# A 3x3 convolution by four columns at a time, with six products each, in a fused convolution, attention and expert kernel

## The chip, the cores and the metric

The kernel runs on one core of one Trainium2 chip. All data is float32. The metric is the device time of one execution, in microseconds, as the median of several runs. The profile is that of one execution; its engines are TensorE (PE, with PEld for its weight loads), VectorE (DVE), ScalarE (ACT), GpSimd (POOL) and SyncE (SP), which only starts transfers.

## The reference

Eight images of 32 x 32 positions with 256 channels pass through two layers. The input of each is normalised first, and its output is added to the input. The first layer is a 3 x 3 convolution to 192 channels beside an attention of 8 heads with relative positions to 64 channels; the second is a plain attention of width 128; after both comes a layer of experts, two of eight per image. Cut to what the change touches:

```
conv_out = lax.conv_general_dilated(x, conv_w, window_strides=(1, 1), padding='SAME', ...) + conv_b
kqv = jnp.einsum('bhwc,co->bhwo', x, qkv_w) + qkv_b
...
return jnp.concatenate([conv_out, attn], axis=3)
...
def _gn(v, G=32, eps=1e-5):
    g = v.reshape(B_, H_, W_, G, C_ // G)
    m = jnp.mean(g, axis=(1, 2, 4), keepdims=True)
    s = jnp.var(g, axis=(1, 2, 4), keepdims=True)
    return ((g - m) / jnp.sqrt(s + eps)).reshape(v.shape)
```

The input of the first layer is normalised over groups of 8 channels (`_gn`). The order of positions matters only to the convolution and the relative positions; every other step treats a position by itself, or sums over all.

## The kernel before

An image is a tile `T` of 128 partitions x 8 tiles x 256 channels, positions on the partitions; two adjacent columns share a partition row (`load_image`, `j=2`). All layers add into `T`.

`norm_steps` transposes `T` to channels on partitions (`xT`), takes mean and variance per channel, averages them over groups by two tiny products, and writes the normalised image with a border of zeros into `gpad` (L319). `by_tiles` copies `gpad` tile by tile into `x` for the products that make the values (L340, GpSimd). `by_pairs` makes the inputs of the convolution: for each pair of output columns and each of two channel halves (`kc`) four differences or sums of neighbouring columns, into `gdif` (L331, two on VectorE and two on GpSimd). `conv_weights` makes four weight variants of the three column taps once, at the start (L273 to L278).

`conv_steps` then runs the convolution of an image as 4 row groups x 2 pairs x 2 variants x 6 products (3 rows x 2 channel halves), 96 calls. Two variants share one PSUM tile `pc`; after the second, VectorE adds them into `T` (first pair: L483 and two L487; second pair: L481). An f32 product is two records in the profile, so 8 images give 1536.

The convolution is a filler for TensorE. An image passes three stages:

- `conv_layer_attention` runs 32 steps of two score products each, per unit of four heads and half the queries. VectorE takes the row maxima of each score tile (`my`, L540, then L544, L547) from one of two PSUM buffers `lg`. After 8 steps of a unit, `fold` (L553 to L558) turns the maxima into a row of the operand `F` by a DMA. From step 10 (`lead = NT + LAG`) `weigh` (L572, then the exponential on ScalarE, L580) and `gather` (L589) run in the same steps. In the first ten steps, when there is nothing to weigh, `conv.run` spreads what is left of the image's calls evenly: `todo = -(-left // (lead - s))`, after a first portion of six.
- After step 32, `ahead` walks through the next image's `norm_steps`, `by_tiles` and `by_pairs`, while the last weights are still gathered. `settle` (L615 to L619) divides by the sums (`rc`, `at`), then come `aT` (L690), `pp` and its addition into `T` (L696).
- `attention_layer` is the second layer. Its `fill` runs `input_steps` of the next image in between (keys and queries `pk` and `kq`, L354 to L366; values `pvv`; the relative products `prel`, L426, with copies L438 and L440), and after each of eight small pieces six calls of the next image's convolution, in the single PSUM buffer `po`.

The order on TensorE is the written one throughout (`tc.manual_schedule`). In the start-up block VectorE's order is the written one as well: normalisation, key patterns, four input steps, `reld_steps`, `by_pairs`, the other input steps, the weights. Elsewhere a scheduler orders each queue at build time[...]. The experts' stage, from about 1985 us on, is not touched but for the shape of its output transfer.

## Time and profile before

| | us |
|---|---|
| median of 3 runs | 2483.72 (2482.58 to 2485.73) |
| the profiled execution | 2482.71 |
| its span, first to last instruction | 2480.2 |
| one image in the steady state (first score to first score) | 242.1 |
| first convolution product of the first image | 58.3 |
| mean granted TensorE clock | 0.984 of full speed |

A group line of the page gives line, engine, operation, output and inputs, shapes and count, then busy time and the mean length of one, then the engine's idle time ahead of it and what ended it. A timeline row gives start, length, engine, line, operation, shapes and how many instructions are merged in it, with the idle time ahead and its end in brackets. A row of busy times by stage gives the stretch, its length, then busy time and instruction count of PE, PEld, DVE, ACT and POOL, the granted clock, the share of the DMA engines and GB/s. A line of waits gives who waited for whom, the sum, the number and the longest.

### The profile page before, as it was taken

To read this page: it belongs to the slowest core of one execution; us is meant where nothing else is said; L and a number is where in the kernel's file an instruction comes from. 1 tells how busy PE (TensorE), PEld (TensorE's weight loads), DVE (VectorE), ACT (ScalarE), POOL (GpSimd) and SP (SyncE) were. 2 spreads that over 40 slices of the span, in tenths; PEclk is the share of its full clock that TensorE was granted. 3 is DMA by queue.
4 is the path that set the end of the run, shared out by engine and by line. 5 is a ranking of instruction groups with operands and counts; after the bars stand their busy time and mean duration, and the time that the engine had idled before them with its cause. 6 is when DMAs were issued, how large, how long until landed. Compare 5 with 4: busy or idle time off the path is not lost. (4 is left out here: it accounts for less than half of the span.)

```text
span 2480.2 us, 42408 instructions
## 1 busy us (share of the span) xinstructions
PE 2362.5 (95%) x17657; PEld 1359.1 (55%) x17657; DVE 1452.0 (59%) x2507; ACT 981.8 (40%) x1625; POOL 449.4 (18%) x463
## 2 busy tenths in 40 slices
PE   5999999999999999999999999999998869999998
PEld 4635753565366436643664376337632646666665
DVE  6774477448744874587368636864674444444443
ACT  1155326432543364336334622472256323322232
POOL 6003020302040103100320122021200132222221
PEclk8999999999999999999999999999999979999999
DMA  4520252024212312241224032402240032211110
GB/s 123 78 41 24 37 101 37 26 44 93 38 37 51 82 30 48 56 77 18 54 54 81 10 57 69 69 5 57 51 71 3 1 124 78 75 68 68 68 60 26
DMA packets 73774, 135.86 MB, mean 55 GB/s; under 512 B 12000, under 2 KB 24168, under 8 KB 71536
## 3 DMA queue, kind: packets, MB, share of 16 engines
q1 hardware_dynamic: 67792, 115.47, 22.7%
q0 software_dynamic: 3056, 15.73, 1.9%
q8 instruction: 139, 2.28, 0.4%
q10 hardware_dynamic: 2736, 1.97, 0.3%
q14 instruction: 51, 0.42, 0.1%
HBM read 53.43 MB, written 25.17 MB: 32 GB/s over the span
## 5 line engine op out<-in xcount | busy, mean ns | idle before, releaser
L580 ACT ACTIVATE PT<-st 128x512 f32<-128x512 f32 (+1 forms) x944 | 541.5, 633 | 580.6 <-PE st L572 576.7
L540 DVE TENSOR_REDUCE my<-lg 128x32 f32<-128x1024 f32 x512 | 617.5, 1222 | 159.7 <-PE st L572 126.5
L572 PE MATMUL st<-F,km 32*128 32x512 f32 x2048 | 550.6, 641 | 14.9 <-DMA F<-mb 8.7
L532 PE MATMUL lg<-km,F 24*128 24x512 f32 x2048 | 525.1, 636 | 0.3 <-issue 0.2
L589 PE MATMUL po<-PT,vall 128*32 128x256 f32 (+1 forms) x3200 | 315.0, 453 | 2.4 <-ACT PT L580 2.4
L472 PE MATMUL pc<-convw,gdif 128*128 128x192 f32 x1536 | 289.0, 337 | 9.7 <-DVE convw L276 6.2
L472 PEld LDWEIGHTS pc<-convw,gdif 128*128 128x128 f32 x1536 | 248.0, 191 | 75.1 <-issue 72.2
L532 PEld LDWEIGHTS lg<-km,F 24*128 24x128 f32 x2048 | 150.9, 183 | 174.3 <-issue 103.2
L589 PEld LDWEIGHTS po<-PT,vall 128*32 128x32 f32 x3200 | 67.0, 108 | 313.9 <-issue 279.9
L572 PEld LDWEIGHTS st<-F,km 32*128 32x128 f32 x2048 | 179.8, 184 | 93.4 <-issue 43.3
L1168 PE MATMUL py<-w,hT 128*128 128x256 f32 x1024 | 223.6, 379 | 0.0
L1151 PE MATMUL phd<-n2T,w 128*128 128x512 f32 x512 | 223.6, 594 | 0.0
L1168 PEld LDWEIGHTS py<-w,hT 128*128 128x128 f32 x1024 | 194.6, 190 | 33.3 <-issue 7.4
L299 POOL TENSOR_TENSOR T<-T,l0b 128x2048 f32<-128x2048 f32 x8 | 36.3, 4536 | 813.2 <-PE tpx L290 813.2
L1151 PEld LDWEIGHTS phd<-n2T,w 128*128 128x128 f32 x512 | 97.0, 191 | 114.8 <-issue 107.7
L1175 DVE TENSOR_TENSOR r<-py,n 128x256 f32<-128x256 f32 x64 | 27.1, 423 | 213.6 <-PE py L1168 213.6
L804 PE MATMUL po<-pt,qkv 128*128 128x256 f32 x512 | 116.6, 381 | 11.3 <-DVE pt L796 11.3
L1158 ACT ACTIVATE hT<-phd,b1c 128x512 f32<-128x512 f32 x128 | 86.3, 686 | 96.4 <-PE phd L1151 96.1
L782 DVE TENSOR_REDUCE nm<-lg 128x1 f32<-128x1024 f32 x64 | 78.2, 1221 | 77.8 <-PE lg L773 77.8
L773 PE MATMUL lg<-qkv 128*128 128x512 f32 x256 | 119.1, 593 | 0.0
L804 PEld LDWEIGHTS po<-pt,qkv 128*128 128x128 f32 x512 | 96.6, 190 | 36.2 <-DVE pt L796 13.2
L721 POOL TENSOR_TENSOR T<-T,n 128x256 f32<-128x256 f32 x64 | 47.2, 744 | 351.8 <-DVE n L716 351.8
(231 smaller groups left out, 2446.5 us busy)
## 6 DMA issues: line engine op xcount, KB each, us to landing
F<-rh SPq DMA_DIRECT2D x256, 128.0 KB
F<-kq SPq DMA_DIRECT2D x256, 64.0 KB
F<-rwd SPq DMA_DIRECT2D x256, 64.0 KB
w<-in_L_ffn_W_dram SPq DMA_DIRECT2D x32, 512.0 KB
rwd<-rw SPq DMA_DIRECT2D x16, 512.0 KB
Td<-T POOLq DMA_DIRECT2D x8, 1024.0 KB, 7.9
T<-Td SPq DMA_DIRECT2D x8, 1024.0 KB
out_dram<-yo SPq DMA_DIRECT2D x16, 512.0 KB
```

Of the source, the lines that this page charges most:

```text
L472: nc.tensor.matmul(pc[:, v, :], lhsT=gflat[:, 2 * pair + v, kc, at : at + P], rhs=convw[:, 2 * pair + v, dy, kc, :], start=i == 0, stop=i ...
L532: nc.tensor.matmul(lg[:, a, :], lhsT=self.F[r : r + 24, a, 0, i * P : (i + 1) * P], rhs=KM[self.g][r : r + 24, a].rearrange("p e k -> p (e ...
L540: nc.vector.tensor_reduce(my[:, :, hl], lg.rearrange("p a (y x) -> p y a x", y=WW), AX.XY, ALU.max)
L572: nc.tensor.matmul(st[:, i, :] if len(heads) > 1 else st, lhsT=KM[self.g][r : r + 32, a, e, :], rhs=self.F[r : r + 32, a, e, :], start=Tru ...
L580: nc.scalar.activation(self.pts[j][:, hs, :], st, AF.Exp)
L589: nc.tensor.matmul(self.po[32 * hl : 32 * hl + 32, cols], lhsT=vall[:, j, h * (DH + 1) : h * (DH + 1) + 32], rhs=self.pts[j][:, hl, cols], ...
L773: nc.tensor.matmul(lg[:, h, :], lhsT=qk[0][:, i * P : (i + 1) * P], rhs=qk[1][:, h * 512 : (h + 1) * 512], start=True, stop=True,)
L782: nc.vector.tensor_reduce(nm, lg, AX.X, ALU.max, negate=True)
L804: nc.tensor.matmul(po[:, 0:IB], lhsT=v1[:, jc, :], rhs=pt[:, jc, :], start=jc == 0, stop=jc == NT - 1)
L1151: nc.tensor.matmul(phd, lhsT=ws[k][0][:, kc, f * P : (f + 1) * P], rhs=n2T[:, kc, q * 512 : (q + 1) * 512], start=kc == 0, stop=kc == KC - 1,)
L1158: nc.scalar.activation(hT[:, k * NF + f, :], phd, AF.Gelu, bias=b1c[:, f, k * B + b : k * B + b + 1])
L1168: nc.tensor.matmul(py, lhsT=hT[:, k * NF + f, j * P : (j + 1) * P], rhs=ws[k][1][:, f, :], start=k == 0 and f == 0, stop=k == TOPK - 1 and ...
```

## The change

The convolution now makes four columns of outputs at a time from six products, where it made two from four; per image 2 row groups x 3 pairs x 2 variants x 6 products, 72 calls. The six weight variants and the six sums of columns have constants other than one, so that the sums are built by multiply-and-add (`scalar_tensor_tensor`) on VectorE and by additions on GpSimd, in two loops (`by_fours`): the first makes variants 0 and 1 out of 2 to 5 as scratch, the second fills 2 to 5 anew. The outputs of a pair of products go through a copy (`neg`) and a sum and difference (`sd`) before they are added to `T`.

Positions lie in tiles of every fourth column (`j=4` in the loads and stores), and the normalised image `x` is kept by columns without a border; the padded copy `gpad` and `by_tiles` are gone, and keys, queries and values read `x`. The order of the keys follows.

```diff
-                out=t.rearrange("p (r j) c -> p r j c", j=2), in_=xt[b].rearrange("(r p j) c -> p r j c", p=P, j=2)
+                out=t.rearrange("p (r j) c -> p r j c", j=4), in_=xt[b].rearrange("(r p j) c -> p r j c", p=P, j=4)
...
-        gpad = wp.tile([P, KC, HH + 2, WW + 2], FP, tag="gpad", name="gpad")
-        nc.gpsimd.memset(gpad, 0.0)
...
-        gdif = wp.tile([P, 4, KC, HH + 2, WW // 2], FP, tag="gdif", name="gdif")
+        NV, NQ = 6, WW // 4
+        gdif = wp.tile([P, NV, KC, HH + 2, NQ], FP, tag="gdif", name="gdif")
...
+            cw = [convw[:, v] for v in range(NV)]
+            nc.vector.tensor_tensor(cw[1], w0, w2, ALU.add)
+            nc.vector.tensor_tensor(cw[0], cw[1], w1, ALU.add)
+            nc.vector.tensor_tensor(cw[1], cw[1], w1, ALU.subtract)
+            nc.vector.tensor_scalar(convw[:, 0:2], convw[:, 0:2], -1.0 / 6, None, ALU.mult)
+            nc.vector.scalar_tensor_tensor(cw[3], w2, 4.0, w0, ALU.mult, ALU.add)
+            nc.vector.scalar_tensor_tensor(cw[2], w1, 2.0, cw[3], ALU.mult, ALU.add)
+            nc.vector.scalar_tensor_tensor(cw[3], w1, -2.0, cw[3], ALU.mult, ALU.add)
+            nc.vector.tensor_scalar(convw[:, 2:4], convw[:, 2:4], 1.0 / 24, None, ALU.mult)
+            nc.scalar.mul(cw[4], w0, 0.25)
+            nc.scalar.copy(cw[5], w2)
...
-                nc.vector.tensor_scalar(
-                    gpad[:, kc, 1 : HH + 1, 1 : WW + 1], xv, gm[:, kc, :], gr[:, kc : kc + 1], ALU.subtract, ALU.mult
-                )
...
+            xn = xn.rearrange("p (k a c j x) -> p k a c j x", k=KC, a=2, j=4, x=16)
             for kc in range(KC):
                 for a in range(2):
...
+                    nc.vector.tensor_scalar(
+                        xn[:, kc, a],
+                        xT[:, kc, a * 512 : (a + 1) * 512].rearrange("p (j x c) -> p c j x", j=4, x=16),
+                        gm[:, kc, :],
+                        gr[:, kc : kc + 1],
+                        ALU.subtract,
+                        ALU.mult,
+                    )
+            held["xn"] = xn
+
+        def by_fours(xn):
...
+            d = [[xn[:, kc, :, :, j].rearrange("p a c x -> p a x c") for j in range(4)] for kc in range(KC)]
+            v = [
+                [gdif[:, i, kc, 1 : HH + 1, :].rearrange("p (a x) c -> p a x c", a=2) for i in range(NV)]
+                for kc in range(KC)
+            ]
+
+            def stt(out, one, factor, two):
+                for a in range(2):
+                    nc.vector.scalar_tensor_tensor(out[:, a], one[:, a], factor, two[:, a], ALU.mult, ALU.add)
+
+            for d_, v_ in zip(d, v):
+
+                stt(v_[2], d_[1], -4.0, d_[3])
+                stt(v_[3], d_[0], -4.0, d_[2])
+                nc.gpsimd.tensor_tensor(v_[4], d_[3], d_[1], ALU.subtract)
+                nc.gpsimd.tensor_tensor(v_[5], d_[2], d_[0], ALU.subtract)
+                nc.gpsimd.tensor_tensor(v_[0], v_[2], v_[3], ALU.add)
+                nc.gpsimd.tensor_tensor(v_[1], v_[2], v_[3], ALU.subtract)
+            for d_, v_ in zip(d, v):
+
+                stt(v_[2], v_[5], 2.0, v_[4])
+                stt(v_[3], v_[5], -2.0, v_[4])
+
+                stt(v_[4], d_[1], -5.0, d_[3])
+                stt(v_[4][:, :, :, 1:NQ], d_[3][:, :, :, 0 : NQ - 1], 4.0, v_[4][:, :, :, 1:NQ])
+                nc.vector.tensor_scalar(v_[5], d_[0], 4.0, None, ALU.mult)
+                stt(v_[5], d_[2], -5.0, v_[5])
+                nc.gpsimd.tensor_tensor(
+                    v_[5][:, :, :, 0 : NQ - 1], v_[5][:, :, :, 0 : NQ - 1], d_[0][:, :, :, 1:NQ], ALU.add
+                )
...
-                    rhs=gpad[:, kc, 1 + 16 * q : 17 + 16 * q, 1 : WW + 1],
+                    rhs=xn[:, kc, q * 512 : (q + 1) * 512],
...
+            for r in range(2):
+                four = T[b][:, 4 * r : 4 * r + 4, 0:CO]
+                for pair in range(3):
...
+                                if pair < 2:
+                                    neg = work.tile([P, CO], FP, tag="neg", name="neg")
+                                    sd = work.tile([P, 2, CO], FP, tag="sd", name="sd", bufs=2)
+                                if pair == 0:
+                                    nc.scalar.copy(neg, pc[:, 1, :])
+                                    nc.vector.tensor_tensor(sd[:, 0], pc[:, 0, :], neg, ALU.add)
+                                    nc.vector.tensor_tensor(sd[:, 1], pc[:, 0, :], neg, ALU.subtract)
+                                    for h in range(2):
+                                        nc.gpsimd.tensor_tensor(
+                                            four[:, 2 * h : 2 * h + 2], four[:, 2 * h : 2 * h + 2], sd, ALU.add
+                                        )
+                                elif pair == 1:
+                                    nc.scalar.mul(neg, pc[:, 1, :], 2.0)
+                                    nc.vector.scalar_tensor_tensor(
+                                        sd[:, 0], neg, 0.5, pc[:, 0, :], ALU.mult, ALU.add
+                                    )
+                                    nc.vector.scalar_tensor_tensor(
+                                        sd[:, 1], pc[:, 0, :], 2.0, neg, ALU.mult, ALU.subtract
+                                    )
+                                    nc.gpsimd.tensor_tensor(four[:, 0:2], four[:, 0:2], sd, ALU.add)
+                                    nc.vector.scalar_tensor_tensor(
+                                        four[:, 2:4], sd, 4.0, four[:, 2:4], ALU.mult, ALU.add
+                                    )
+                                else:
+                                    nc.vector.tensor_tensor(four[:, 0:4:3], pc, four[:, 0:4:3], ALU.add)
...
-                self.left = 4 * NT // 2 * 3 * KC if b < B else 0
+                self.left = 2 * NV * 3 * KC if b < B else 0
...
-            by_pairs()
+            by_fours(held["xn"])
...
-                    yield from norm_steps(b + 1)
-                    held.update(by_tiles())
-                    by_pairs()
+                    yield from norm_steps(b + 1, held)
+                    by_fours(held["xn"])
```

More of the change, by code (lines that the diff above doesn't have):

```diff
@@ L271, in conv_weights, with norm_steps @@
             taps = taps.rearrange("p (a b n) -> p b a n", a=3, b=3)
-            convw = wp.tile([P, 4, 3, KC * CO], FP, tag="convw", name="convw")
-            nc.vector.tensor_tensor(convw[:, 2], taps[:, 0], taps[:, 2], ALU.add)
-            nc.vector.tensor_tensor(convw[:, 0], convw[:, 2], taps[:, 1], ALU.add)
-            nc.vector.tensor_tensor(convw[:, 1], convw[:, 2], taps[:, 1], ALU.subtract)
-            nc.vector.tensor_scalar(convw[:, 0:2], convw[:, 0:2], 0.5, None, ALU.mult)
-            nc.scalar.copy(convw[:, 2], taps[:, 0])
-            nc.scalar.mul(convw[:, 3], taps[:, 2], -1.0)
+            w0, w1, w2 = (taps[:, i] for i in range(3))
+            convw = wp.tile([P, NV, 3, KC * CO], FP, tag="convw", name="convw")
+            cw = [convw[:, v] for v in range(NV)]
[9 more added lines that the diff above has]
+            nc.scalar.copy(cw[5], w2)
             return convw.rearrange("p v a (k o) -> p v a k o", o=CO)
-        def norm_steps(b):
+        def norm_steps(b, held):
             xT = pt_tile("xT").rearrange("p (k s) -> p k s", k=KC)
@@ L290, in norm_steps @@
                     nc.tensor.transpose(tp[:, t, :], T[b][:, t, kc * P : (kc + 1) * P], ident)
-                nc.vector.tensor_copy(
-                    xT[:, kc, :].rearrange("p (r t j) -> p r j t", r=4, j=2), tp.rearrange("p (r j) t -> p r j t", j=2)
-                )
+                nc.vector.tensor_copy(xT[:, kc, :], tp.rearrange("p t k -> p (t k)"))
                 for q in range(2):
@@ L316, in norm_steps @@
             nc.vector.reciprocal(gr, gr)
-            for kc in range(KC):
-                xv = xT[:, kc, :].rearrange("p (h w) -> p h w", w=WW)
-                nc.vector.tensor_scalar(
-                    gpad[:, kc, 1 : HH + 1, 1 : WW + 1], xv, gm[:, kc, :], gr[:, kc : kc + 1], ALU.subtract, ALU.mult
-                )
-        def by_pairs():
-            for kc in range(KC):
-                d = [gpad[:, kc, 1 : HH + 1, j : j + WW - 1 : 2] for j in range(4)]
-                for v, (one, two, op) in enumerate(
-                    ((1, 2, ALU.add), (2, 1, ALU.subtract), (0, 2, ALU.subtract), (1, 3, ALU.subtract))
-                ):
-                    eng = nc.vector if v < 2 else nc.gpsimd
-                    eng.tensor_tensor(gdif[:, v, kc, 1 : HH + 1, :], d[one], d[two], op)
@@ L333, in by_tiles @@
-        def by_tiles():
             xn = f_tile("x").rearrange("p a e s -> p (a e s)")[:, 0 : KC * S]
-            xn = xn.rearrange("p (k j t) -> p k j t", k=KC, j=NT)
+            xn = xn.rearrange("p (k a c j x) -> p k a c j x", k=KC, a=2, j=4, x=16)
             for kc in range(KC):
                 for a in range(2):
-                    for e in range(4):
-                        nc.gpsimd.tensor_copy(
-                            xn[:, kc, a * 4 + e].rearrange("p (y x) -> p x y", y=8),
-                            gpad[:, kc, 1 + 16 * a : 17 + 16 * a, 1 + 8 * e : 9 + 8 * e],
-                        )
-            return dict(xn=xn)
+                    nc.vector.tensor_scalar(
[6 more added lines that the diff above has]
+                    )
@@ L346, in input_steps @@
         def input_steps(b, held):
+            xn = held["xn"].rearrange("p k a c j x -> p k (a c j x)")
             kq = work.tile([P, S], FP, tag="kq", name="kq")
@@ L363, in input_steps @@
                 nc.scalar.activation(
-                    kq[qs, q * 512 : (q + 1) * 512], pk[qs], AF.Identity, bias=kqbs[qs], scale=kqs[qs]
-                )
-                nc.vector.tensor_scalar(
-                    kq[0:DK, q * 512 : (q + 1) * 512].rearrange("p (e y x) -> p x e y", e=4, y=8),
-                    pk[0:DK].rearrange("p (x e y) -> p x e y", e=4, y=8),
-                    kqb[0:DK],
-                    None,
-                    ALU.add,
-                )
+                    kq[qs, q * 512 : (q + 1) * 512].rearrange("p (x y) -> p x y", y=WW),
+                    pk[qs].rearrange("p (y x) -> p x y", y=WW),
+                    AF.Identity,
+                    bias=kqbs[qs],
+                    scale=kqs[qs],
+                )
+                nc.vector.tensor_scalar(kq[0:DK, q * 512 : (q + 1) * 512], pk[0:DK], kqb[0:DK], None, ALU.add)
             for g in range(NG):
@@ L388, in input_steps @@
                         pv[:, j, :],
-                        lhsT=held["xn"][:, kc, j, :],
+                        lhsT=xn[:, kc, j * P : (j + 1) * P],
                         rhs=qkvw[:, kc, 2 * DK : 3 * DK],
@@ L463, in conv_steps @@
             n = 3 * KC
-            for r in range(NT // 2):
-                both = T[b][:, 2 * r : 2 * r + 2, 0:CO]
-                for pair in range(2):
+            for r in range(2):
+                four = T[b][:, 4 * r : 4 * r + 4, 0:CO]
+                for pair in range(3):
                     pc = place[0]("pc")[:, 0 : 2 * CO].rearrange("p (v o) -> p v o", v=2)
@@ L470, in conv_steps @@
                             dy, kc = divmod(i, KC)
-                            at = (8 * r + dy) * (WW // 2)
+                            at = (16 * r + dy) * NQ
                             nc.tensor.matmul(
@@ L479, in conv_steps @@
                             if v and i == n - 1:
-                                if pair:
-                                    nc.vector.tensor_tensor(both, pc, both, ALU.add)
-                                else:
-                                    nc.vector.tensor_tensor(
-                                        both, both, pc[:, 0:1, :].to_broadcast([P, 2, CO]), ALU.add
-                                    )
-                                    for j, op in enumerate((ALU.add, ALU.subtract)):
-                                        nc.vector.tensor_tensor(both[:, j], both[:, j], pc[:, 1, :], op)
+                                if pair < 2:
+                                    neg = work.tile([P, CO], FP, tag="neg", name="neg")
+                                    sd = work.tile([P, 2, CO], FP, tag="sd", name="sd", bufs=2)
@@ L606, in close @@
                 nc.scalar.copy(
-                    self.os.rearrange("p (r j t) -> p r j t", r=2, j=2),
-                    self.po.rearrange("p (r t j) -> p r j t", r=2, j=2),
+                    self.os.rearrange("p (j t) -> p j t", j=4), self.po.rearrange("p (t j) -> p j t", j=4)
                 )
@@ L898 @@
             half_w, half_h, reld_steps = tables()
-            for _ in norm_steps(0):
+            for _ in norm_steps(0, held):
                 pass
-            held.update(by_tiles())
             KM = key_patterns()
@@ L923, in ahead @@
                 def ahead():
-                    yield from norm_steps(b + 1)
-                    held.update(by_tiles())
-                    by_pairs()
+                    yield from norm_steps(b + 1, held)
+                    by_fours(held["xn"])
                 now, held = held, {}
@@ L1184 @@
             nc.sync.dma_start(
-                out=ot[b, q * 512 : (q + 1) * 512, :].rearrange("(r p j) c -> p r j c", p=P, j=2),
-                in_=y.rearrange("p (r j) c -> p r j c", j=2),
+                out=ot[b, q * 512 : (q + 1) * 512, :].rearrange("(p j) c -> p j c", j=4),
+                in_=y,
             )
```

## The prediction

> **What bounds the kernel now.** I read the page first, then the busy time by stage, the waits of single stages, and the timelines of VectorE and GpSimd where the change falls. The page:

> ```profile
> PE 2362.5 (95%) x17657; PEld 1359.1 (55%) x17657; DVE 1452.0 (59%) x2507; ACT 981.8 (40%) x1625; POOL 449.4 (18%) x463
> L472 PE MATMUL pc<-convw,gdif 128*128 128x192 f32 x1536 | 289.0, 337 | 9.7 <-DVE convw L276 6.2
> ```

> TensorE looks like the bound, at 95%, and the convolution (L472) has 1536 of its records, two for each f32 product. But "busy" stretches over waits inside a pipelined group, and the share is a mean over stages. An image takes 242 us, and its convolution is spent in two places: half fills the attention layer before (48 calls), half fills the ten steps in which only scores run (the lead: 560 to 594 us for the second image, 62 to 106 us for the first, which has all 96 calls there). By stage (columns: length, then busy time of PE, PEld, DVE, ACT, POOL):

> ```profile
> 62.00:106.00 44.00, 43.78 (x266) 32.98 (x264) 33.03 (x47) 0.00 (x0) 0.00 (x0) 0.99 0.50 68
> 560.00:594.00 34.00, 33.87 (x181) 20.08 (x182) 30.74 (x46) 1.49 (x2) 13.35 (x17) 1.00 0.41 100
> 691.00:708.00 17.00, 14.78 (x100) 4.12 (x92) 5.70 (x10) 14.48 (x21) 10.65 (x20) 1.00 0.00 0
> ```

> The second row matters most: in a later lead VectorE works 30.74 of 34.00 us. The waits of that stretch say who waits:

> ```profile
> PEld lg L532 <- DVE my L540: 4.4, 10, 0.8
> DVE my L540 <- PE lg L532: 2.2, 5, 0.6
> ```

> The score products wait for the maxima (L540) to free their two buffers more than the reverse. So the later leads are nearly bound by VectorE; only the first, with 33.03 of 44, is bound by TensorE. The tail of the attention, where the next image is normalised:

> ```profile
> 692.58 1.54 DVE L319 TENSOR_SCALAR gpad<-xT,gm,gr 128x1024 f32<-128x1024 f32 x2
> 694.03 2.97 DVE L331 TENSOR_TENSOR gdif<-gpad 128x512 f32<-128x512 f32 x4
> 706.86 0.26 DVE L618 RECIPROCAL rc<-pa 128x16 f32<-128x16 f32 x1 [9.85 <-PE pa L615]
> 707.15 0.29 DVE L619 TENSOR_TENSOR at<-pa,rc 128x128 f32<-128x128 f32 x1
> 707.36 1.48 DVE L690 COPY aT<-tpa 64x512 f32<-64x512 f32 x2
> ```

> From the start of the normalisation to the reciprocal (L618) VectorE has 706.86 - 692.58 = 14.28 us, 9.85 of them idle. From L618 on TensorE, in its written order, stands behind VectorE (at, aT, then pp). This is the cover that new VectorE work may use up. Start-up:

> ```profile
> 28.03 5.59 DVE L238 TENSOR_TENSOR reld<-bdh 128x192 f32<-128x192 f32 x8
> 33.54 4.32 DVE L331 TENSOR_TENSOR gdif<-gpad 128x512 f32<-128x512 f32 x4
> 37.78 1.06 DVE L366 TENSOR_SCALAR kq<-pk,kqb 64x512 f32<-64x512 f32 x1
> 38.69 0.66 DVE L395 TENSOR_TENSOR vall<-pvv,vb 128x512 f32<-128x512 f32 x1
> 39.28 1.87 DVE L438 COPY rw<-prel 128x512 f32<-128x512 f32 x2
> ```

> Here VectorE's order too is the written one: whatever the differences cost is passed to the rw copies, to the products after them, and to the first convolution at 58.25 us.

> [...]in the last stage four STT, 0.48 us each alone, took 2.15 us each beside GpSimd additions:

> ```profile
> 2073.12 8.60 DVE L1181 SCALAR_TENSOR_TENSOR yo<-r,fmv,T 128x256 f32<-128x256 f32 x4
> 2076.42 2.53 POOL L1141 TENSOR_TENSOR n<-n,bias 128x1024 f32<-128x1024 f32 x1
> ```

> That is one VectorE instruction per GpSimd instruction. [...]L547, reading 128 elements in steps of 16 bytes, takes 381 ns, L544 with 128 contiguous ones 293.[...]

> **The change part by part.**

> *Products.* 96 calls an image become 72: 24 x 2 records x 8 = 384 records fewer. A record costs 0.172 us (12 of them between 232.64 and 234.70 us in TensorE's timeline), so 8.26 us an image, 66 us in all, if TensorE were everywhere the bound. The attention layer still runs eight times six calls, so all 24 go from the lead, whose calls after the first six go from 42 to 18.

> *The later leads (seven).* VectorE's part of the convolution there was 3.5 us (L481 2 x 0.55, L483 2 x 0.55, L487 4 x 0.34). Left are one middle pair (two STT of 192 from PSUM, 0.41 each from L820's 0.479 for 256, and one of 384 in SBUF, 0.61 from L1180's 0.484 plus 128 ns) and one last pair (0.55): 2.0. But the old last pair came behind the fold (L553 to L558), whose DMA opens the next stage; the new one falls in front of it. Up to the fold VectorE goes from 2.9 to 2.0, less 0.3 for waits beside GpSimd's token sum. I take -0.6 an image, -4 in all; bounds -2 each (if TensorE's remaining stalls go too) and +0.5.

> *The first lead.* TensorE's step falls from 1.07 + 9 x 0.344 = 4.2 us to 3.3; VectorE's step (two maxima 2.36, folding 0.33, evictions about 0.55, gaps) is 3.4 to 3.6. -6 rather than -8.3. The four further weight operations (4 x 1.36 as L273 to L276, 5.4 us more on VectorE) lie beside the 5.6 us that it waited before its first maximum at 63.73, and cost nothing while the first pair waits only for its own two variants; otherwise +5.

> *Tail.* Removed: two L319, four L331, and on GpSimd 16 copies (6.6 us) and four differences. Added on VectorE: four TENSOR_SCALAR of 512 reading every eighth element, about 0.57 (L319 has 0.77 for 1024), 2.3; 28 STT of 128 elements. An STT of 128 is L1180's 0.484 - 0.128 = 0.36, 0.29 from start to start; 20 of them read d, in steps of 256 bytes, at 0.38; two TENSOR_SCALAR 0.35 each. Own time 2.3 + 8 x 0.29 + 20 x 0.38 + 0.7 = 12.9 us. GpSimd: eight additions of 256 in the first loop at 0.73 (L721) and two at the end. Now in order: at 3.8 us the first four STT are done beside the first two GpSimd ones; six more GpSimd ones at 0.78 go to 8.6, and let six STT through; left are 6 x 0.29 + 12 x 0.38 + 0.7 = 7.0, and one wait of 0.6: 16.2 us. Cover 14.28: L618 comes 1.9 us late, and TensorE with it. Six images like this, and the first pass with 15.8 of cover (449.00 to 464.76) 0.4: +12. Lower bound 0[...]; upper about 6 each, 40 in all[...].

> *Start-up.* The first eight STT go from 33.5 to 36.6. GpSimd's key patterns, ahead in its queue, end near 37 (41.3 less 4.4 for the copies that go); four additions to 39.9, and only then may the second loop overwrite. It ends near 49.5 (3.0 with one STT per GpSimd operation, 2.6, and 3.8 for the other half) where it ended at 37.8: +11 with L366's contiguous form 0.4 shorter. Bounds +6 and +14.

> *Attention layer.* A first or middle pair frees the single po buffer after one ScalarE copy (0.32) and two VectorE operations (0.7 to 0.8), about what three took before (1.2); a middle pair had 0.55. The 1.5 us of prel and tpn products between calls cover that, where ScalarE isn't in a copy. +1, bounds -2 and +7. GpSimd's additions into T come behind its own T additions; the DMA shapes (4 KB runs for 2 KB) wait for nothing here.

> *Sum:* 11 - 6 - 4 + 12 + 1 = +14. On the profiled execution (2482.71 us, its span 2480.2) 2496.7; the runs' median is 1.0 above it: 2498.

> **Rivals.**

> *The differences weigh more* (2533): stall 5.9 in six tails and 4.4 in one (+40), start-up +14, leads 0, first lead -6, layer +1: +49. For it: 28 small strided instructions beside ten GpSimd ones. Against: GpSimd's copies beside L331 barely slowed it (0.74 for 0.69).

> *The cover holds* (2468, faster): VectorE finishes within 14.28 us of the normalisation's start, so tails cost 0; start-up +6, first lead -8, seven leads -2: -16. It decides if the 28 STT average under 0.40 us as issued, waits included: (14.28 - 2.3 - 0.7) / 28. For it: 9.85 us idle; against: L1181.

> *Products count in full* (2418): all 66 us. For it: the 95%. Against: the waits in the later leads.

> **How the numbers follow.** Chances: my forecast 0.48 (own range 2487 to 2512), heavier 0.17, cover holds 0.25, full 0.06, else 0.04. The range 2466 to 2532 leaves out half of the heavier case, the full one and a little of each other. About 0.2% (5 us) is what a measurement of this kernel tells from no change. Faster: nearly all of cover and full, less their edge, 0.27; within: 0.13; slower: 0.60.

> **What would show it.** Later leads about as long as before with VectorE over 93% busy; L618 late and its idle time before it gone; the first convolution near 69 us; the first lead 6 us shorter. Wrong, if the leads shrink by several us each (then TensorE did bound them), or if VectorE is idle again before L618.

## The result, and the profile after

The kernel after the change takes 2580.01 us (median of 4 runs, 2577.76 to 2585.70) against 2484.64 us before: a ratio of 1.0388, 95% interval 1.0370 to 1.0407. It is slower, by nearly seven times the difference that was forecast. The profiled execution took 2577.76 us, with a span of 2576.0, so 95.8 us more span than before. The page of the kernel after:

```profile
PE 2423.9 (94%) x17273; PEld 1361.3 (53%) x17273; DVE 1532.9 (60%) x2703; ACT 992.2 (39%) x1657; POOL 503.2 (20%) x430
...
PEclk6999989998999799969996999699989879999999
...
L571 PE MATMUL lg<-km,F 24*128 24x512 f32 x2048 | 596.0, 735 | 6.7 <-DVE my L579 6.6
L611 PE MATMUL st<-F,km 32*128 32x512 f32 x2048 | 579.5, 671 | 15.5 <-DMA F<-mb 10.2
L494 PE MATMUL pc<-convw,gdif 128*128 128x192 f32 x1152 | 250.2, 364 | 7.5 <-DVE convw L276 6.3
```

The records of the convolution are down from 1536 to 1152, as they should be. But TensorE is busy for 61 us *more* (2423.9 against 2362.5), and the products that the change doesn't touch are longer: a score product (L571, L532 before) takes 735 ns on average where it took 636, a product of the weights' scores (L611) 671 where it took 641. The row PEclk says why: the granted clock dips in each of images 2 to 8, to 6 or 7 tenths in four of them. Its mean is 0.924 of full speed, 0.984 before. One image of each kernel by stage; in a row stand the length, then the busy time (and records) of PE, PEld, DVE, ACT, POOL, then the granted clock, the DMA share and GB/s. After, from the first score product of the fifth image: lead, steady stage, tail (from the next image's normalisation to its key products), the attention layer up to its own query and key products, and the rest of that layer.

```profile
1085.36:1125.17 39.81, 39.30 (x129) 19.62 (x130) 28.89 (x40) 1.82 (x3) 14.30 (x18) 0.57 0.35 84
1125.17:1229.54 104.37, 103.20 (x805) 37.34 (x802) 73.15 (x99) 61.14 (x109) 4.57 (x1) 0.94 0.27 43
1229.54:1251.24 21.70, 16.88 (x100) 7.30 (x101) 18.65 (x38) 12.92 (x19) 11.23 (x10) 0.92 0.00 1
1251.24:1290.40 39.16, 38.70 (x681) 33.42 (x681) 16.37 (x43) 10.20 (x18) 14.89 (x14) 0.96 0.35 68
1290.40:1344.72 54.32, 51.32 (x239) 36.27 (x237) 25.49 (x56) 19.64 (x34) 1.11 (x2) 1.00 0.21 33
```

The same image before:

```profile
1044.20:1077.92 33.72, 33.63 (x179) 19.84 (x178) 30.46 (x45) 1.49 (x2) 13.35 (x17) 1.00 0.40 100
1077.92:1176.76 98.84, 97.69 (x801) 34.88 (x802) 72.58 (x98) 60.91 (x109) 4.54 (x1) 1.00 0.28 45
1176.76:1194.20 17.44, 15.22 (x100) 5.67 (x100) 6.22 (x10) 12.93 (x19) 10.63 (x20) 1.00 0.01 2
1194.20:1231.94 37.74, 37.10 (x681) 32.77 (x681) 17.00 (x43) 9.45 (x15) 10.40 (x9) 1.00 0.34 72
```

The lead has 50 TensorE records fewer (48 by the code) and is 6 us longer; the steady stage has the same work on every engine and is 5.5 us longer. In both the clock has gone down, and no other column has grown to match. The stages of all images summed, in us:

| | start to first score | 8 leads | 7 steady stages | 7 tails | 7 layers, first part | second part | rest | span |
|---|---|---|---|---|---|---|---|---|
| before | 62.4 | 280.2 | 691.8 | 123.6 | 266.0 | 380.2 | 676.0 | 2480.2 |
| after | 72.3 | 292.4 | 724.9 | 149.5 | 276.4 | 380.2 | 680.3 | 2576.0 |
| difference | +9.9 | +12.2 | +33.1 | +25.9 | +10.4 | 0 | +4.3 | +95.8 |

The trace's records of the granted clock have two values, 1.0 and 0.5. Around the fourth and fifth image (start and length in us, factor):

```
before   946 to 1287: always 1.0
after    841.5  37.5  0.5    lead and steady stage of image 4
         879.0 109.2  1.0
         988.3   6.8  0.5    tail of image 4
         995.1  95.6  1.0
        1090.7  47.8  0.5    lead and steady stage of image 5
        1138.4 109.2  1.0
        1247.7   6.8  0.5    tail of image 5
```

The leads whose clock was low for long (images 4 to 7) are 37.4 to 39.8 us long, those where it was low only in the last ten us or less (images 2, 3 and 8) 32.7 to 33.1, where before had 33.8. In all seven VectorE runs the same instructions in the same order. So the theory to be tested: the convolution in the lead was not only work, it kept TensorE's clock up. With 18 calls left of 42 the clock falls to half there and stays low into the next stage. Its rival: VectorE's added work is the loss, and the low clock only mirrors a TensorE that waits.

### The profile page after: what moved, and what is told of

Its sections match the earlier page's. It is cut to its first block, busy times and chain, and to the rows that moved or that the text cites. A ratio compares the mean times of both kernels' runs of the same rounds, so it can differ in the third digit from the quotient of the medians.

```text
span 2576.0 us, 41839 instructions
## 1 busy us (share of the span) xinstructions
PE 2423.9 (94%) x17273; PEld 1361.3 (53%) x17273; DVE 1532.9 (60%) x2703; ACT 992.2 (39%) x1657; POOL 503.2 (20%) x430
## 5 line engine op out<-in xcount | busy, mean ns | idle before, releaser
L619 ACT ACTIVATE PT<-st 128x512 f32<-128x512 f32 (+1 forms) x944 | 543.1, 633 | 531.6 <-PE st L611 521.4
L571 PE MATMUL lg<-km,F 24*128 24x512 f32 x2048 | 596.0, 735 | 6.7 <-DVE my L579 6.6
L611 PE MATMUL st<-F,km 32*128 32x512 f32 x2048 | 579.5, 671 | 15.5 <-DMA F<-mb 10.2
L628 PE MATMUL po<-PT,vall 128*32 128x256 f32 (+1 forms) x3200 | 320.8, 461 | 2.9 <-ACT PT L619 2.4
L571 PEld LDWEIGHTS lg<-km,F 24*128 24x128 f32 x2048 | 177.3, 209 | 199.4 <-issue 110.5
L494 PE MATMUL pc<-convw,gdif 128*128 128x192 f32 x1152 | 250.2, 364 | 7.5 <-DVE convw L276 6.3
L494 PEld LDWEIGHTS pc<-convw,gdif 128*128 128x128 f32 x1152 | 200.9, 205 | 99.3 <-issue 94.0
L611 PEld LDWEIGHTS st<-F,km 32*128 32x128 f32 x2048 | 190.5, 191 | 90.8 <-issue 42.0
L820 DVE TENSOR_REDUCE nm<-lg 128x1 f32<-128x1024 f32 x64 | 78.1, 1221 | 77.8 <-PE lg L811 77.8
L842 PEld LDWEIGHTS po<-pt,qkv 128*128 128x128 f32 x512 | 96.6, 190 | 36.3 <-DVE pt L834 13.2
```

Of the source, the lines that this page charges most:

```text
L494: nc.tensor.matmul(pc[:, v, :], lhsT=gflat[:, 2 * pair + v, kc, at : at + P], rhs=convw[:, 2 * pair + v, dy, kc, :], start=i == 0, stop=i ...
L571: nc.tensor.matmul(lg[:, a, :], lhsT=self.F[r : r + 24, a, 0, i * P : (i + 1) * P], rhs=KM[self.g][r : r + 24, a].rearrange("p e k -> p (e ...
L611: nc.tensor.matmul(st[:, i, :] if len(heads) > 1 else st, lhsT=KM[self.g][r : r + 32, a, e, :], rhs=self.F[r : r + 32, a, e, :], start=Tru ...
L619: nc.scalar.activation(self.pts[j][:, hs, :], st, AF.Exp)
L628: nc.tensor.matmul(self.po[32 * hl : 32 * hl + 32, cols], lhsT=vall[:, j, h * (DH + 1) : h * (DH + 1) + 32], rhs=self.pts[j][:, hl, cols], ...
L820: nc.vector.tensor_reduce(nm, lg, AX.X, ALU.max, negate=True)
```

## The experiments

Twelve kernels were made from these two; where nothing else is said, the edit is one of the kernel after. "Step" is a call of the convolution: one f32 product, two records.

**Filling the lead with unused products.** In the steps that have no weights' scores, if `b`:

```diff
+        def idle(calls):
+            dum = st_tile("dum")
+            for i in range(calls):
+                nc.tensor.matmul(dum[:, 0:CO], lhsT=gflat[:, 0, 0, 0:P], rhs=convw[:, 0, 0, 0, :], ...)
...
                     conv.run(todo)
                     left -= todo
+                    if b:
+                        idle(4 + 2 * (s in (0, 1, 8, 9)))
```

> The changed kernel with 48 extra products of the convolution's shape (results not used) in the lead of each image but the first, as many as the change took out of the lead. Theory 1 (the granted clock): the lead's thinner filler lets TensorE's clock fall to half for 24 to 48 us an image; with the extra products the lead and the steady stage run at full clock, leads of images 3 to 6 come back to about 33 us and the stage from the first exponential's statistics to the normalisation from 104.4 to about 99 us, together some 55 to 70 us: 2510 to 2525. Theory 2 (VectorE's extra work is the loss, the low clock only shows that TensorE waits): TensorE is given work that nobody needs, nothing is gained: 2575 or more.

It took 2538.96 us, 41 less than the kernel after, but above the range of theory 1. The seven steady stages are back (691.6 us together), the clock is 1.00 in them, yet a lead is 38.0 us. Its row shows why:

```profile
1072.70:1110.70 38.00, 38.00 (x227) 27.00 (x226) 31.02 (x41) 1.82 (x3) 14.57 (x18) 1.00 0.35 89
```

TensorE is busy for the whole 38.00 us. The expectation misjudged the dose: 48 products are 96 records, twice the 24 products that the change took out, and they now bound the lead. (Two more steps at the end of the tail also get unused products, 8 here, 4 in `idle_24`, 2 in `idle_12`.) So the right dose, `idle(2 + (s in (0, 1, 8, 9)))`, and half of that, `idle(1 + (s in (0, 9)))`:

> The changed kernel with 24 unused products in the lead of each image but the first. A product shows as two matmuls in the trace, so this is exactly what the change took out of the lead (48 matmuls), half of what the run idle_lead put in, where TensorE was busy for all of the 38.0 us of a lead. Theory 1 (the granted clock): leads of 33 to 34 us, the stage after them 98.8 us in all seven images, 2510 to 2525, under idle_lead's 2539. Theory 2 (what idle_lead won has another cause than the clock): no better than idle_lead, 2539 or more.

> As idle_24 with 12 unused products in a lead in place of 24. Theory 1, with a bound of activity between the two: either the clock holds already (leads 33 us, 2512 to 2520) or it falls in some images (2525 to 2570); each stage that is long is one with half clock beside it. Theory 2: no relation between the half clock and the stage lengths.

They took 2514.46 us (1.0135 of before, 1.0118 to 1.0152) and 2516.92 us (1.0149, 1.0124 to 1.0174). The fifth image's lead and steady stage with 12 products:

```profile
1066.94:1099.80 32.86, 31.52 (x156) 16.43 (x155) 30.23 (x43) 1.82 (x3) 14.50 (x18) 1.00 0.41 105
1099.80:1198.72 98.92, 97.79 (x801) 34.61 (x802) 71.65 (x95) 60.92 (x109) 4.57 (x1) 1.00 0.29 45
```

More work for TensorE, useless work, and the lead is 7 us shorter and the stage behind it 5.5. Nothing else in these stages was changed: in the traces of `idle_12` and of the kernel after, VectorE, ScalarE and GpSimd run the same instructions in the same order from start to end. So the rival falls. By medians the clock in the leads and the stages behind them is worth 2580.0 - 2516.9 = 63 us, two thirds of the loss.

**The reverse: the kernel before, with less work in the lead.** Every second product is left out in each lead but the first image's, so what the kernel computes is not the convolution; the evictions stay.

```diff
+                            half = b and place[0] is st_tile
+                            if not (half and i % 2):
                                 nc.tensor.matmul(
...
-                                    stop=i == n - 1,
+                                    stop=i == (n - 2 if half else n - 1),
```

> The kernel before with every second product of the convolution left out in the lead of every image but the first (its results are then not those of the reference; evictions are all kept, so VectorE, ScalarE and GpSimd do what they did). Theory 1: with less work TensorE's clock falls to half in the lead and after it, and the kernel gets slower by some 40 to 70 us, 2525 to 2555, though only work was taken away. Theory 2: 0 to 6 us faster, since those products hid beside VectorE.

It took 2517.44 us, 1.0130 of before (1.0113 to 1.0147): slower by 34 us with work taken away, less than the 40 to 70 expected. The fifth image's lead, 33.72 us in the kernel before:

```profile
1065.00:1105.70 40.70, 39.39 (x140) 19.70 (x139) 32.16 (x49) 1.49 (x2) 13.89 (x17) 0.62 0.34 86
```

The low clock costs 7 us here, but it had mostly come back by the end of the lead (the steady stages are 696.0 us together, 4 more than before, not 33), which is where the expectation was too high. None of the change's edits is in this kernel, so they aren't needed for the effect.

**Useful work in place of unused: three steps at each place in the attention layer instead of six.** 48 of the 72 steps are then left to the lead, 24 in the kernel after.

```diff
-                            conv.run(6)
+                            conv.run(3)
```

> The changed kernel with three convolution steps instead of six at each place in the attention layer's fill, so that 48 of an image's 72 steps are left for the next lead (18 in the changed kernel, 42 in the kernel before). Theory 1: the lead is back at full clock (55 to 70 us won), and the attention layer, which TensorE bounds, is shorter by 24 to 30 steps of 0.5 us, some 8 us in up to seven images: 2455 to 2475. Theory 2: the attention layer's share alone, 2520 to 2545, with leads no shorter than now.

It took 2476.36 us, just above its range, 0.9969 of before (0.9957 to 0.9980): with this the changed kernel is faster than the one before, by 0.3%. The same image's lead and the first part of its layer:

```profile
1032.64:1066.61 33.97, 33.75 (x179) 19.85 (x179) 30.39 (x44) 2.14 (x4) 16.67 (x20) 1.00 0.41 100
...
1185.43:1217.32 31.89, 30.86 (x633) 25.65 (x633) 15.49 (x40) 9.69 (x17) 13.56 (x12) 0.95 0.27 70
```

The lead is as long as before, at full clock, with the 24 products hidden in it; the layer, which TensorE bounds (30.86 of 31.89), is 7.3 us shorter for them, 0.30 us each (the 0.5 expected was an estimate). Here, not in the lead, a removed product is worth its time.

**The tail.** The first part of its reading, from the kernel after's VectorE timeline (start and length in us), and from its waits:

```profile
1229.54 3.49 DVE L324 TENSOR_SCALAR x<-xT,gm,gr 128x512 f32<-128x512 f32 x4
1232.94 6.28 DVE L345 SCALAR_TENSOR_TENSOR gdif<-x 128x128 f32<-128x128 f32 x8
...
1246.42 0.25 DVE L656 RECIPROCAL rc<-pa 128x16 f32<-128x16 f32 x1
```

```profile
PE tpa L727 <- DVE at L657: 2.8, 1, 2.8
```

From the normalisation to the reciprocal VectorE now needs 1246.42 - 1229.54 = 16.88 us without a pause; TensorE waits 2.8 us for it, and then has half clock for 6.8. The 16 small products behind (`pp`), after and then before, with minimum, median and maximum ns:

```profile
L733 PE MATMUL pp<-aw,aT x16: 417/417/469, 1247.6 to 1250.9; 64*128 64x64 f32 x16
```

```profile
L695 PE MATMUL pp<-aw,aT x16: 272/272/320, 1192.3 to 1194.0; 64*128 64x64 f32 x16
```

Can the wait be filled? `idle_lead` with `idle(8)` behind the transposes of the last unit:

> As the run before it, and 8 more unused products behind the transposes of the last unit of an image, where TensorE waits 2.8 us for VectorE and its clock is at half for 6.8 us afterwards. Theory 1: the wait is filled, the half clock behind it goes, products of the token stage fall back from 3.7 to 2.0 us, some 3 to 4 us an image: 2485 to 2495. Theory 2 (rival: the tail is late because VectorE is, whatever TensorE does): no difference from the run before it, within 5 us.

It took 2549.83 us, 11 more than `idle_lead`: neither. `idle_lead` already had unused products there, and TensorE no wait of that length any more; sixteen together outlast the wait, and TensorE, with hardly a gap, became the bound of the tail (21.7 us where `idle_lead` had 20.7).

Can VectorE's second loop in `by_fours` move out of the way? First by its place in the text alone, `by_fours` called in two parts, the second behind `conv_layer_attention`:

> The changed kernel with the second loop of by_fours issued behind the convolution layer's tail (after the attention product is added to T) instead of ahead of the last unit's reciprocal, in the seven later images. Theory 1: TensorE's wait for VectorE in the tail (2.8 us) and the half clock of 6.8 us behind it go, normalisation to key products falls from 21.5 to about 17.5 us and the layer from 39.5 to about 38.5: some 25 to 35 us in all, 2545 to 2555; leads stay at half clock. Rival (the low clock of the lead is all that counts, the second loop is only moved into the attention layer and costs there what it cost before): within 6 us of 2580.

> Both edits: three convolution steps at each place (2476 us in the run three) and the second loop of by_fours behind the tail. Theory 1: another 20 to 28 us off, 2448 to 2456. Rival as for tail_split: 2470 to 2480.

They took 2572.42 us (2567.04 to 2584.52) and 2475.58 us, as the kernels without the edit. The edit did nothing at all: VectorE's order isn't the written one here, and in the traces VectorE, ScalarE and GpSimd run the same instructions in the same order as without it. Both count as repeats of the kernel after and of `three`. As a repeat the first is of use: its leads are 37.3 to 37.9 us long in images 2, 5 and 8 and 32.7 to 33.5 in the others, so the same program loses its clock early in other images from run to run. A dependence then forced the order, in place of the factors 2 and -2:

```diff
+                nc.vector.tensor_scalar(two, behind, 0.0, 2.0, ALU.mult, ALU.add)
+                nc.vector.tensor_scalar(minus, behind, 0.0, -2.0, ALU.mult, ALU.add)
...
-                stt(v_[2], v_[5], 2.0, v_[4])
-                stt(v_[3], v_[5], -2.0, v_[4])
+                stt(v_[2], v_[5], two, v_[4])
+                stt(v_[3], v_[5], minus, v_[4])
...
+            if b:
+                by_fours(held["xn"], 2, kq[:, S - 1 : S])
```

> The changed kernel; the second loop of by_fours of the seven later images multiplies by two factors that are made from the last column of kq, so that VectorE can't begin it before the tail's reciprocal, aT and the key products are through (in tail_split, where only its place in the text was moved, VectorE's order stayed as in the changed kernel). Leads stay as they are. Theory 1: TensorE's wait of 2.8 us in the tail and the 6.8 us of half clock behind it go, normalisation to key products falls from 21.5 to about 17.5 us, and the layer loses no more than it had: 2548 to 2558. Rival (the second loop costs in the layer what it cost in the tail): within 6 us of the changed kernel's 2578.

2599.79 us, 20 more than the kernel after. The fifth image's tail and layer, and TensorE's longest wait in that layer (the traced run is the fastest of the four, 2589.96 us):

```profile
1238.65:1256.09 17.44, 15.22 (x100) 5.67 (x100) 11.53 (x16) 12.93 (x19) 8.50 (x8) 1.00 0.01 1
1256.09:1300.98 44.89, 40.58 (x681) 34.94 (x681) 23.75 (x67) 10.18 (x18) 18.43 (x16) 0.92 0.33 61
```

```profile
PE tpn L766 <- DVE n L762: 3.9, 1, 3.9
```

The tail is as long as before the change, 17.44 us, at full clock: the second loop does cause what the tail lost. But the loop now stands in VectorE's queue ahead of the normalised tiles `n`, TensorE waits for those, its clock falls there, and the layer pays 5.7 us for 4.3 won. The rival was nearer, and even it too low.

**Versions meant to be faster.** At start-up, the second loop and the weights of products 3 and 4 behind the first two weights, with `three` (its split of the tail has no effect):

> As three_tail, and at start-up the second loop of by_fours and the weights of products 3 and 4 come behind the weights of products 1 and 2, with which the first convolution begins. The start-up term of the prediction (11 us, VectorE's added work ahead of the first convolution) would fall to some 4 us: 2441 to 2450. Rival (start-up waits for something else, the weights of the relative tables or a DMA): as three_tail.

2470.50 us (2460.53 to 2472.51), 0.9945 of before (0.9924 to 0.9966): the fastest of all, though above its range, since the split of the tail that the range counted on is void, and not clearly apart from `three` (2467.43 to 2479.04). TensorE's waits at start-up, of the kernel after and of this one:

```profile
PE prel L447 <- ACT rw L461: 14.4, 1, 14.4
PE pc L494 <- DVE convw L276: 6.3, 1, 6.3
```

```profile
PE pc L497 <- DVE convw L276: 6.3, 1, 6.3
```

The wait of 14.4 us for the copies `rw` is gone (VectorE's copies stood behind `by_fours` in its queue, until 48.99 us, and ScalarE's waited 22.4 us for VectorE's); the first score product comes at 58.0 us for 72.6. Of these 14.6 us the first lead gives half back (43.9 us for 36.6).

That kernel with the dependence of `tail_late`, and then with the second loop in eight pieces, one behind each tile `n`, and the convolution's pairs as the outer loop:

> three_tail_start with that tail: 20 to 28 us under it by theory 1, 2442 to 2452; by the rival 2465 to 2475.

> all_three with the second loop of by_fours cut in eight pieces, one behind each normalised tile n of the attention layer, and with the convolution's three pairs as its outer loop, so that the 24 steps in the attention layer use only products 1 and 2 and no step waits for the second loop. Theory: in tail_late and all_three the second loop (7.3 us) stood in VectorE's queue ahead of the attention layer's own tiles and cost what the tail had won; spread over VectorE's idle half of that layer it costs at most 1 to 3 us an image: normalisation to key products 17.4, the layer 32 to 35 us against 39.8, 2445 to 2465. Rival (the layer has no room for it): 2490 or more.

2522.60 and 2492.00 us (1.0172 with 1.0134 to 1.0211, and 1.0031 with 1.0020 to 1.0041): the first above both its ranges, the second as its rival said. The runs of `all_three` scatter from 2498.51 to 2533.01 us, and its trace is of the fastest. In their traces both win in the tail (17.4 to 19.1 us) and lose more in the layer, 32 to 33 us in `three`, 39.8 and 36.3 to 39.4 here. The spread layer of the fifth image, and in it two of the pieces and the addition of GpSimd beside them:

```profile
1195.83:1233.86 38.03, 32.08 (x633) 26.90 (x633) 30.30 (x69) 9.92 (x17) 16.18 (x15) 0.91 0.31 68
...
1224.49 4.77 DVE L348 SCALAR_TENSOR_TENSOR gdif<-x,gdif 128x128 f32<-128x128 f32 x2
1224.29 4.54 POOL L783 TENSOR_TENSOR T<-T,bo 128x2048 f32<-128x2048 f32 x1
```

VectorE's 15.49 us of this stage in `three` became 30.30 for a loop of 7.3: beside GpSimd's additions into `T` the pieces are longer (the last two took 4.77 us, where the same two took 0.65 in the tail of the kernel after). My theory of an idle half that would take it in was wrong. TensorE's longest waits in this layer are 3.8 us for ScalarE's `nT` and 2.2 for VectorE; how they share the loss was not taken apart.

## Why the prediction was wrong

The direction was right and the size was not. Step by step:

- *Start-up, +11:* 9.9, the first convolution at 68.2 us ("near 69"). Right.
- *First lead, -6:* 43.87 to 37.25 us, -6.6. Right.
- *Later leads, "I take -0.6 an image, -4 in all; bounds -2 each ... and +0.5".* This is the step that failed. Its arithmetic holds where the clock holds: -0.7 to -1.1 in images 2, 3 and 8, -1.1 each over the seven leads of `idle_12`. But the step counted what the fewer products cost and free as work on engines, and took the length of each record as given. In images 4 to 7 the leads grew by 3.6 to 6.1 us, and the seven steady stages, for which the prediction had no term since nothing in them is edited, by 33.1. The runs put a product count to it: with 12 unused products a lead all of that is gone.
- *Tails, +12:* 25.9. VectorE's chain was sized well as a whole (16.88 us for 16.2), in part by luck: its four normalising instructions took 3.49 us where 2.3 were put. (The 1 ns an element in the forecast's prices was an estimate; before, the 192 elements more of L481 than of L487 take 551 - 346 = 205 ns. The bounds, 0 and about 6 us a tail, were estimates that no trace shows.) So the reciprocal is 2.6 us late, for 1.9. Mis-sized was what follows: TensorE works on after its wait of 2.8 us at half clock, and seven tails cost 3.7 us each instead of 1.7 (by these figures the late reciprocals are some 18 of the 25.9 us, the half clock the rest).
- *Attention layer, +1:* 10.4. This too is the half clock, which reaches from the tail into the layer. The kernel `idle_lead` shows it, in which the seven layers are the same but for the clock. Its second and third image (6 us at half clock, and none):

```profile
479.43:519.91 40.48, 40.02 (x682) 33.88 (x681) 16.36 (x43) 10.21 (x18) 14.88 (x14) 0.93 0.34 66
731.61:769.16 37.55, 37.09 (x681) 32.79 (x681) 16.16 (x43) 10.17 (x18) 14.88 (x14) 1.00 0.36 71
```

  Its seventh, with 3.0 us at half clock, takes 38.99. At full clock the layer is no longer than before (37.74 in the fifth image), so the evictions that the term was about cost nothing here.
- *Rivals.* All three had only work and waits in them; the heaviest, 2533, missed by 47 us. "Products count in full" fails in the leads, but `three` shows the place where products do count: the layer.
- *What would show it:* the reciprocal late and its idle time gone, as said. The later leads were not over 93% VectorE; 28.89 of 39.81 us is 73%, and that low share beside a longer stage was the sign that a third thing bounded it. (Even in image 3, where the lead was short, it is 28.67 of 32.79, 87%.)

An estimate from these figures of what the change costs with the clock at full throughout: start-up +9.9, leads -14.4 (265.8 us together in `idle_12`, for 280.2), seven tails of 2.6 us +18, layers -3 (seven of 37.55, for 266.0), about +11 in all. The forecast of +14 is near that, but leads and tails miss by 4 and 6 us in opposite directions, so part of the nearness is luck. No kernel was run in that state: those with 12 and 24 unused products, still with half clock in tails and layers, are 32 to 34 us above before.

## What to carry to other kernels

Before taking work from TensorE in a stage that another engine bounds, look at the granted clock there and at how close together TensorE's records stand. Here, in the fifth image, 12 unused products beside VectorE went with a clock of 1.00 in the lead and in the stage behind it, where the kernel after had 0.57 and 0.94; over all images they were worth 63 us. Take removed products from a stage that TensorE bounds (24 of them, 7.3 us of the layer of `three`), and leave the filler where the gaps are. An edit of the text alone moved no instruction on VectorE where its order isn't the written one (`tail_split`), and a loop moved out of the tail's way was paid for in the layer: 5.7 us for 4.3 won in `tail_late`.

## What the runs showed of the hardware

In the records of the kernels before and after (16 and 40) the clock has two values, 1.0 and 0.5, and changes only in steps of about 3.41 us: every length (3.4, 6.8, 13.7, 37.5, 47.8 us, but not the last of each kernel, which the end cuts off) is a multiple of it, within rounding. What sends the clock down they do not say. The kernel after in windows of that length, around a fall at 1090.70:

```profile
1083.87:1087.29 3.42, 3.42 (x22) 2.19 (x20) 2.53 (x9) 0.21 (x1) 1.72 (x3) 1.00 0.82 166
1087.29:1090.70 3.41, 2.90 (x12) 1.26 (x12) 3.33 (x5) 0.00 (x0) 3.06 (x4) 0.99 0.94 257
1090.70:1094.11 3.41, 3.41 (x13) 1.47 (x12) 2.14 (x4) 0.00 (x0) 3.13 (x4) 0.50 0.53 154
```

In the window before the fall TensorE shows 2.90 of 3.41 us busy, and its longest wait is 0.5 us; in the leads of images 3 to 8 no wait is longer than that either, and no pause of the weight loads is over 1.5 us. The window has 12 records. In the leads of the kernel before, the same kind of window (cut as the clock's own records are) never has fewer than 16.

There is no sharp line. Two windows of the kernel after, in the second and the fourth image; the clock held after the first and fell after the second, at 841.5:

```profile
332.90:336.31 3.41, 3.05 (x14) 1.17 (x14) 3.27 (x6) 0.51 (x1) 3.15 (x4) 1.00 0.53 67
838.07:841.48 3.41, 3.05 (x14) 1.17 (x14) 3.27 (x6) 0.39 (x1) 3.08 (x4) 1.00 0.53 70
```

The thinnest window of `idle_12`'s fifth lead, where the clock held:

```profile
1076.95:1080.36 3.41, 2.94 (x14) 1.25 (x10) 3.31 (x4) 0.00 (x0) 3.12 (x4) 1.00 0.54 64
```

```profile
1042.90:1046.31 3.41, 2.33 (x7) 0.79 (x6) 2.50 (x3) 1.21 (x2) 0.00 (x0) 1.00 0.21 25
```

Neither modelled busy time nor weight loads (PEld) separate the windows that fell from those that held (3.05 and 1.17 us in both of the two above). What the clock goes by, and why it then stays low for up to 47.8 us here and for 3.4 elsewhere, stays open.
